# A prologue of its own for the first batch of a four-layer cross-attention kernel: the order of the first projections, the first maxima and the weights

## The chip, the core and the metric

The kernel runs on one core of a Trainium2 chip. The core has five engines, each with an instruction queue of its own: TensorE (PE, with its weight loads as PEld), VectorE (DVE), ScalarE (ACT), GpSimd (POOL) and SyncE (SP), which only issues DMAs here. ACT and POOL can issue DMAs too, and an issue takes its place in their queues. Every engine works through its queue in order and waits on semaphores for what another engine or a DMA has to deliver.

The metric is the time of one execution on the device in microseconds, the median of several runs. Profile times are microseconds from the start of the profiled span unless they are marked ns.

## The reference

`x` has shape (2, 1024, 288): two batches of 1024 tokens. It goes through two quantised layers, L0 and L1, and two plain layers, L2 and L3, which attend to 154 context rows. Only the beginning of L0 matters for this change:

```python
h = layer_norm(x, ln1_g, ln1_b, 1e-06)
q8, s, sm = quant_act(h)
q = quant_linear(q8, s, sm, wq1, bq1).reshape(b, n, H, D)   # H = 16 heads, D = 18
k = quant_linear(q8, s, sm, wk1, bk1).reshape(b, n, H, D)
v = quant_linear(q8, s, sm, wv1, bv1).reshape(b, n, H, D)
a = attn(q, k, v)
a8, sa, sma = quant_act(a)
x = x + quant_linear(a8, sa, sma, wo1, bo1)
...
```

`quant_act` rounds each token to integers in -127..127 by its own scale, and `quant_linear` quantises each weight row to 8 bits before it multiplies. A cross-attention and a feed-forward part follow in L0 and L1.

## The kernel before

**Tiles.** A batch has two halves of 512 tokens (`HQ`), each of four chunks of 128 tokens. The 16 heads are worked in four groups of four (`G`). One *step* of self-attention is one group of one half of one batch of one layer, so that there are 32 steps, eight for each batch of a layer.

**A step.** `self_maxima` (lines 558 to 585) finds the row maxima of the logits first: 32 units, each a matmul of 128 queries against 512 keys (line 564) and a DVE maximum over them (line 571). `store_maxima` (lines 530 to 552) splits the maxima into three bf16 parts on POOL, transposes them and puts them as extra rows into the query tile by a DMA that ACT issues. Only then can `attend` form the products: logits with the maxima already in them (`weights_unit`, line 623), the exponential on ACT (line 629) and the product with the values (line 653). `run` (line 783) lays the maxima of step i + 1 between the products of step i; the maxima of step 0 have nothing beside them.

**What a batch needs first.** `SelfAttention.prepare` (line 874) does for each half: `ln_quantise` (line 376: statistics on DVE, normalisation on ACT, the multiplication by g and addition of b on POOL at line 401, quantisation on DVE and ACT with small columns on POOL), `transposed`, `token_scales`, then keys, values and queries. Keys and queries go through `linear_T` (line 513), in three tiles of 108 features: three matmuls, a scaling on DVE (line 520), and `split` (line 473), which takes a number apart into three bf16 parts in the order ACT, POOL, ACT, POOL. `put` (line 492) writes the parts to DRAM, and `get_group` (line 504) reads them back, 72 features of a group at a time. The tile of the parts has two buffers.

**The order around the change.** The end of `tile_xattn` (lines 1427 to 1475) sets it. Before any step, three things are emitted to their end: `prep_a` (the norm's rows and the weights of keys, values and queries, line 832), `prep_a_out` (the output weight, line 841) and `layers[0].prepare()` (keys, values and queries of both halves). `self_attention` then fetches keys and two query tiles, and runs. All later work of other layers and batches is *side* work, which `beside` (line 1403) lays between the steps by weights: side work with weights of 118 in all, spread over 112 of the 128 yields of the first eight steps. The first entry of that side work is `layers[1].prepare()`, the second batch.

This order is only a priority. A planner (`schedule_with_timeline_sim`, line 56) simulates the engines and moves later work into gaps that it expects, within the limits of buffers and dependencies. The queues that the chip sees are its result.

**Loads.** SP issues all 16 chunks of `x` first (lines 109 and 110), and the weights and biases after them. POOL issues the context, the norm's rows and more. The rows of ones in the two key tiles `kT` are written by POOL (`head_rows`, line 87, called at line 1432).

Of the kernel before, what the change touches and what calls it, by code (L numbers as in the profile page):

```python
# [10 lines left out]
F32 = mybir.dt.float32  # L11
# [41 lines left out]
def tile_xattn(ctx: ExitStack, tc: tile.TileContext, ins: dict, out: bass.AP):  # L53
# [40 lines left out]

    def pair_rows(kt):

        ktv = kt.rearrange("p (q j) t -> p q j t", j=2)
        for q in range(H // 2):
            for n, (k0, k1) in enumerate(((0, NTXT), (NTXT, T))):
                nc.gpsimd.tensor_copy(  # L100
                    ktv[96:P, q, :, k0:k1],
                    ones22[96:P, :, n : n + 1].to_broadcast([P - 96, 2, k1 - k0]),
                )


# [3 lines left out]
    for n in range(NCH):  # L109
        nc.sync.dma_start(out=x[:, n, :], in_=xd[:, n, :])  # L110
# [168 lines left out]
    def prep(W, w_name, b_name, row0=0):  # L279
# [6 lines left out]
        nc.sync.dma_start(  # L286
# [8 lines left out]
    def prep_T(W, w_name, b_name, scaled=False):  # L295
# [6 lines left out]
        for n, f in enumerate(FT):  # L302
            nc.sync.dma_start(out=wv[:, n, :], in_=ins[w_name][f : f + FR, :])
# [72 lines left out]
    def ln_quantise(c0, ln, eps, s, name):  # L376
# [14 lines left out]
        h = view(big(f"{name}h"), c=HC, w=C)  # L391
# [8 lines left out]
        for j, op in ((0, ALU.mult), (1, ALU.add)):  # L400
            nc.gpsimd.tensor_tensor(
                h, h, ln[:, j : j + 1, :].to_broadcast([P, HC, C]), op
            )
        q = view(bf(f"{name}q")[:, 0 : HC * CZ], c=HC, w=CZ)
# [3 lines left out]
    def transposed(q, name):  # L408

        qT = view(bf(f"{name}qT")[:KZ], k=3, t=HQ)  # L410
# [62 lines left out]
    def split(y, bias, nt, name):  # L473

        st = work.tile([FR, 3, HQ], BF16, tag="parts", name=f"{name}st")[:, :, 0:nt]
        if bias is None:
            nc.scalar.copy(st[:, 0, :], y)
            nc.gpsimd.tensor_tensor(y, y, st[:, 0, :], ALU.subtract)
# [13 lines left out]
    def put(rows, st, n, nt):  # L492
        skip = 2 * D if n == 2 else 0
        nc.sync.dma_start(
# [18 lines left out]
    def linear_T(qT, w, sb, rows, name):  # L513

        qw, col = w
        for n in range(3):
# [6 lines left out]
            put(rows, split(y, None, HQ, name), n, HQ)  # L523
            yield 2
# [109 lines left out]

    def follow(one, other):

        one, other = (getattr(i, "ins", i) for i in (one, other))
        tc.add_manual_dep(
            one,
            other.name,  # L640
            mybir.DependencyInfo(
                mybir.DependencyClass.NoSync, mybir.DependencyReason.DATA
            ),
            reason="kept together",
        )
# [222 lines left out]
    class SelfAttention:  # L868
# [5 lines left out]
        def prepare(self):  # L874
            w, b, name = self.w, self.b, self.name
            self.k = [new_rows(f"{name}kr{hf}", "krows") for hf in range(2)]
            self.q = [new_rows(f"{name}qr{hf}", "qrows") for hf in range(2)]
            self.v = dram.tile([S // P, P, VW], F32, tag="vrows", name=f"{name}vr", bufs=2)
            for hf in range(2):
# [7 lines left out]
                yield from linear_T(qT, w["k"], sb, self.k[hf], f"{name}k")  # L887
                for c in range(HC):
                    n = hf * HC + c
                    v = vstage[n % 2]  # L890
                    quant_linear(
                        qT, c, w["v"], s[:, c : c + 1], v_heads(v), f"{name}v", heads
                    )
                    nc.sync.dma_start(out=self.v[n], in_=v)
                yield 3
                yield from linear_T(qT, w["q"], sb, self.q[hf], f"{name}q")
# [19 lines left out]
    def self_attention(layers):  # L916
# [18 lines left out]
        fetch(1)  # L935
        steps = []
        for n, (i, g, hf) in enumerate(order):
            L = layers[i]

            def pre(n=n, i=i, g=g, hf=hf, L=L):  # L940
                if g == 0:
# [40 lines left out]
        return run(steps)  # L982
# [23 lines left out]
    def cross_attention(w, b, name):  # L1006
# [38 lines left out]
        def queries(hf):  # L1045
# [7 lines left out]
            yield from linear_T(qT, w["q"], sb, rows[hf], f"{name}q")  # L1053
# [345 lines left out]
    def weighed(gen):  # L1399
        for _ in gen:  # L1400
            yield 1

# [24 lines left out]
    with tc.tile_pool(name="apool", bufs=1) as apool:  # L1427
        WA, WO = Weights(tpool, 1, 3, 1), Weights(apool, 1, 1, 1)
        kts = []
        for n, pool in enumerate((tpool, apool)):  # L1430
            kt = pool.tile([P, 4, S], BF16, name=f"kT{n}")
            head_rows(kt, 4, S)
            kts.append(kt)
        vstage = []
        for n in range(2):
# [6 lines left out]
        drain(prep_a(L0, wa[0]))  # L1442
        drain(prep_a_out(L0, wa[0]))
        drain(layers[0].prepare())
        main = self_attention(layers)
        sides = (
            (chain(layers[1].prepare(), prep_b(L0, wb[0]), prep_c(L0, wc[0])), 118),
# [21 lines left out]
        beside(main, 24, chain(islice(last, 2), weighed(islice(plain, 21))), 25, 24)  # L1469
# [47 lines left out]
```

## Time and profile before

| what | value |
|---|---|
| median of 3 runs | 2659.57 us (2655.34 to 2670.14) |
| the profiled execution, as timed | 2656.43 us |
| its profiled span | 2654.5 us |
| mean granted TensorE clock in it | 0.855 |
| PE busy in the span | 2057.5 us (78%) |
| DVE busy in the span | 1971.1 us (74%) |
| ACT busy in the span | 1409.9 us (53%) |
| POOL busy in the span | 819.3 us (31%) |
| first product of step 0 (line 623) starts | 160.9 us |
| first product of step 8 starts | 446.0 us |
| first product of step 16 starts | 954.5 us |

Busy times are the sums of an engine's instructions. Timeline rows read: start, length, engine, line, operation, written tile `<-` read tiles, shape, count; in brackets the idle time before it and what ended it. A row with a count above one is a merged run of neighbours. In names, `L_xattn_a` stands for the self-attention of any quantised layer, so that a row does not tell the batch or layer. In the window table each engine has its busy time and its count of instructions, followed by the granted TensorE clock, the busy share of the DMA engines and GB/s.

### The profile page before, as it was taken

The numbers are of one execution on the slowest core, as the hardware profiler recorded it, in microseconds if no ns is written. First come the engines' busy times: TensorE is split into PE (matmuls) and PEld (weight loads), VectorE is DVE, ScalarE is ACT, GpSimd is POOL, SyncE is SP. The second block draws the span as 40 slices with busy tenths as digits, with TensorE's granted clock in tenths as the row PEclk, the third lists the DMA queues.
The fourth block names the chain that finished last, engine by engine and source line by source line (L and its number), as shares of the span: only waits on it lengthen the run. The fifth ranks groups of instructions, "written<-read, shape, count | busy, mean of one in ns | idle before, by whom it ended". The sixth has DMA issues, their size and how long they took to land. (4 is left out here: it accounts for less than half of the span.)

```text
span 2654.5 us, 34216 instructions
## 1 busy us (share of the span) xinstructions
PE 2057.5 (78%) x10908; PEld 907.0 (34%) x10908; DVE 1971.1 (74%) x4512; ACT 1409.9 (53%) x2707; POOL 819.3 (31%) x1804
## 2 busy tenths in 40 slices
PE   1488998787884887788768677787767887778898
PEld 0223332323332333233333232323334433444444
DVE  6687888788888477888868958897357876655666
ACT  2346556555664755566656354466654544544443
POOL 7524212402124442022253440123264122413220
PEclk9779888789986888989868778798888977879999
DMA  3422201220000312110023121100033210112321
GB/s 88 122 70 86 57 22 49 77 55 17 27 11 20 119 44 78 42 29 21 6 83 94 31 80 34 33 23 12 25 82 101 74 28 25 51 40 67 86 66 36
DMA packets 158340, 140.27 MB, mean 53 GB/s; under 512 B 44251, under 2 KB 154164, under 8 KB 158161
## 3 DMA queue, kind: packets, MB, share of 16 engines
q1 hardware_dynamic: 147152, 118.67, 15.4%
q0 software_dynamic: 4864, 14.71, 2.3%
q10 hardware_dynamic: 6144, 4.72, 1.0%
q8 instruction: 86, 1.41, 0.2%
q14 instruction: 94, 0.76, 0.1%
HBM read 95.27 MB, written 38.04 MB: 50 GB/s over the span
## 5 line engine op out<-in xcount | busy, mean ns | idle before, releaser
L571 DVE TENSOR_REDUCE L_xattn_amxh<-L_xattn_amx 128x1 f32<-128x512 f32 x1024 | 670.9, 680 | 131.2 <-PE L_xattn_amx L564 123.7
L629 ACT ACTIVATE L_xattn_aatse<-L_xattn_aats 128x512 f32<-128x512 f32 x1024 | 556.1, 600 | 281.2 <-PE L_xattn_aats L623 245.1
L564 PE MATMUL L_xattn_amx<-kT,L_xattn_aqT 108*128 108x512 bf16 x1024 | 425.2, 433 | 122.1 <-DVE L_xattn_amxh L571 91.8
L623 PE MATMUL L_xattn_aats<-L_xattn_aqT,kT 120*128 120x512 bf16 x1024 | 374.7, 413 | 49.8 <-ACT L_xattn_aatse L629 33.4
L653 PE MATMUL L_xattn_aato<-L_xattn_aatse,L_xattn_av 128*32 128x512 f32 x2048 | 288.0, 634 | 22.1 <-ACT L_xattn_aatse L629 18.3
L629 ACT ACTIVATE L_xattn_atse<-L_xattn_ats 86x512 f32<-86x512 f32 (+1 forms) x256 | 139.7, 590 | 121.9 <-PE L_xattn_ats L623 98.5
L623 PEld LDWEIGHTS <-kT 120*128 120x128 bf16 x1024 | 98.9, 103 | 304.3 <-issue 262.0
L564 PEld LDWEIGHTS <-L_xattn_aqT 108*128 108x128 bf16 x1024 | 104.5, 105 | 266.7 <-issue 221.5
L627 DVE TENSOR_TENSOR L_xattn_batse<-L_xattn_bats,L_xattn_bmT 77x512 f32<-77x512 f32 x256 | 166.6, 676 | 37.1 <-PE L_xattn_bats L623 26.5
L629 ACT ACTIVATE L_xattn_batse<-L_xattn_batse 77x512 f32<-77x512 f32 x256 | 155.1, 622 | 37.8 <-DVE L_xattn_batse L627 32.2
L609 DVE TENSOR_REDUCE L_xattn_mxn<-L_xattn_mx 128x2 f32<-128x172 f32 (+1 forms) x512 | 129.3, 304 | 50.4 <-PE L_xattn_mx L594 48.3
L1280 PE MATMUL L_xattn_o<-wo,L_xattn_atp 128*128 128x288 f32 x512 | 143.7, 424 | 4.3 <-ACT L_xattn_mxsr L545 1.8
L604 DVE TENSOR_TENSOR L_xattn_bmxm<-L_xattn_bmx,L_xattn_bm 128x308 f32<-128x308 f32 x256 | 114.6, 464 | 30.8 <-PE L_xattn_bmx L594 25.8
L623 PE MATMUL L_xattn_bats<-L_xattn_bqT,L_xattn_bkT 120*77 120x512 bf16 x256 | 96.7, 433 | 42.0 <-DMA L_xattn_bqT<-L_xattn_bmxsr 29.0
L188 POOL CAST L_xattn_bmxst<-L_xattn_bmxn 128x16 bf16<-128x16 f32 x96 | 20.4, 212 | 345.4 <-DVE L_xattn_bmxn L609 176.2
L623 PE MATMUL L_xattn_ats<-L_xattn_qT,L_xattn_kT 120*86 120x512 bf16 (+1 forms) x256 | 92.5, 422 | 32.0 <-DMA L_xattn_qT<-L_xattn_mxsr 23.5
L609 DVE TENSOR_REDUCE L_xattn_bmxn<-L_xattn_bmxm 128x2 f32<-128x308 f32 x256 | 113.6, 458 | 0.8
L1280 PEld LDWEIGHTS L_xattn_o<-wo,L_xattn_atp 128*128 128x128 f32 x512 | 97.4, 196 | 38.1 <-DVE L_xattn_atp L764 3.6
L594 PE MATMUL L_xattn_mx<-L_xattn_kT,L_xattn_qT 108*128 108x154 bf16 x512 | 79.0, 257 | 26.3 <-DVE L_xattn_mxn L609 11.5
L594 PE MATMUL L_xattn_bmx<-L_xattn_bkT,L_xattn_bqT 108*128 108x154 bf16 x512 | 81.1, 261 | 21.7 <-DVE L_xattn_amxh L571 6.9
L653 PEld LDWEIGHTS L_xattn_aato<-L_xattn_aatse,L_xattn_av 128*32 128x32 f32 x2048 | 41.8, 110 | 155.8 <-ACT L_xattn_aatse L629 129.8
L594 PEld LDWEIGHTS <-L_xattn_bqT 108*128 108x128 bf16 x512 | 49.5, 110 | 99.3 <-issue 69.8
(558 smaller groups left out, 3848.6 us busy)
## 6 DMA issues: line engine op xcount, KB each, us to landing
kT<-L_xattn_akr SPq DMA_DIRECT2D x192, 72.0 KB
L_xattn_aqT<-L_xattn_aqr SPq DMA_DIRECT2D x192, 72.0 KB
L_xattn_bqT<-L_xattn_bqr SPq DMA_DIRECT2D x192, 72.0 KB
L_xattn_qT<-L_xattn_r SPq DMA_DIRECT2D x192, 72.0 KB
L_xattn_akr<-L_xattn_akst SPq DMA_DIRECT2D x16, 324.0 KB
L_xattn_aqr<-L_xattn_aqst SPq DMA_DIRECT2D x16, 324.0 KB
L_xattn_bqr<-L_xattn_bqst SPq DMA_DIRECT2D x16, 324.0 KB
L_xattn_r<-L_xattn_qst SPq DMA_DIRECT2D x16, 324.0 KB
```

Source lines behind the costliest of these rows:

```text
L188: eng.tensor_copy(part, r)
L564: nc.tensor.matmul(sp, lhsT=qt[:KR, j, c * P : (c + 1) * P], rhs=kt[:KR, j, a * 512 : (a + 1) * 512], start=True, stop=True,)
L571: nc.vector.tensor_reduce(halves[:, a, c, j, :], sp, AX.X, ALU.max, negate=True)
L594: nc.tensor.matmul(sp[:, j * T : (j + 1) * T], lhsT=qt[:KR, 2 * a + j, c * P : (c + 1) * P], rhs=kt[:KR, 4 * g + 2 * a + j, :], start=True ...
L604: nc.vector.tensor_tensor(lm, of, mask[:, c : c + 1, :].to_broadcast([P, 2, T]), ALU.add)
L609: nc.vector.tensor_reduce(nm[:, c, 2 * a : 2 * a + 2, n], of[:, :, k0:k1], AX.X, ALU.max, negate=True,)
L623: nc.tensor.matmul(sp, lhsT=keys(j), rhs=qt[:rows, j, :], start=True, stop=True)
L627: nc.vector.tensor_tensor(e, sp, maskT, ALU.add)
L629: nc.scalar.activation(e, src, AF.Exp)
L653: made = nc.tensor.matmul(po[32 * i : 32 * i + 32, :], lhsT=lhsT, rhs=rhs, start=start, stop=stop)
L1280: nc.tensor.matmul(ps, lhsT=pair[:, c * P : (c + 1) * P], rhs=wo[:, t0 + t, :], start=(t == 0), stop=(t == len(pairs) - 1),)
```

## The change

The first batch of L0 gets a method of its own, `prepare_first`, in place of `prep_a`, `prep_a_out` and `prepare`. It emits: the norm of half 0, the key weight, the transposes of half 0, the norm of half 1, the query weight, keys and queries of half 0, keys of half 1. What is left (`others`: value weight, values of both halves, queries of half 1) is laid between the 32 maxima of step 0, which now yield. The output weight becomes the first entry of the side work, whose weights rise from 118 to 126. Four things change for this batch alone:

- The norm's multiplication and addition and the subtractions in `split` are done by DVE (`nc.vector`) and not by POOL.
- The key and query weights are loaded through ACT's queue.
- The rows of ones in `kT` are written by ACT, eight copies of 32 x 1024.
- SP loads only the eight chunks of the first batch at the start. The second batch's eight chunks are placed behind the last `put` of the keys of half 1.

The norm's result and the transposed integers of this batch also live in other buffers (tags `a` and `qTb` in place of `big` and `bf`). The second query tile is fetched in step 0's `pre` and no longer before the first maxima.

```diff
+    def first_rows(kt):
+        for j in range(4):
+            nc.scalar.copy(kt[96:P, j, :], ones4[96:P, j : j + 1].to_broadcast([P - 96, S]))
...
-    for n in range(NCH):
-        nc.sync.dma_start(out=x[:, n, :], in_=xd[:, n, :])
+    def load_tokens(b, behind=None):
+        for n in range(b * 8, b * 8 + 8):
+            load = nc.sync.dma_start(out=x[:, n, :], in_=xd[:, n, :])
+            if behind is not None:
+                follow(load, behind)
+
+    load_tokens(0)
...
         for j, op in ((0, ALU.mult), (1, ALU.add)):
-            nc.gpsimd.tensor_tensor(
+            eng.tensor_tensor(
...
-            nc.gpsimd.tensor_tensor(y, y, st[:, 0, :], ALU.subtract)
+            eng.tensor_tensor(y, y, st[:, 0, :], ALU.subtract)
...
+        def prepare_first(self):
+            w, b, name = self.w, self.b, self.name
+            self.begin()
+            w["ln"] = load_ln(WA, L0, 1)
...
+            names = [(f"{L0}w{part}1", f"{L0}b{part}1") for part in "kqv"]
+            normalise(0)
+            w["k"] = prep_T(WA, *names[0], queue=nc.scalar)
+            qTs = [transposed(qs[0], f"{name}t", tile())]
+            normalise(1)
+            w["q"] = prep_T(WA, *names[1], scaled=True, queue=nc.scalar)
+            linear(0, "k", self.k)
+            linear(0, "q", self.q)
+            qTs.append(transposed(qs[1], f"{name}t", tile()))
+            load_tokens(1, linear(1, "k", self.k)[-1])
+
+            def others():
+                w["v"] = prep(WA, *names[2])
+                yield 8
+                for hf in range(2):
+                    self.values(hf, qTs[hf], scales[hf])
+                    yield 3
+                linear(1, "q", self.q)
+                yield 6
+
+            return others()
...
         fetch_keys(0)
         fetch(0)
-        fetch(1)
...
             def pre(n=n, i=i, g=g, hf=hf, L=L):
+                if n == 0:
+                    fetch(1)
...
-        return run(steps)
+        return run(steps, first=1)
...
-            head_rows(kt, 4, S)
+            first_rows(kt)
...
-        drain(prep_a(L0, wa[0]))
-        drain(prep_a_out(L0, wa[0]))
-        drain(layers[0].prepare())
+        others = layers[0].prepare_first()
         main = self_attention(layers)
+        beside(main, 33, others, 20, 30)
         sides = (
-            (chain(layers[1].prepare(), prep_b(L0, wb[0]), prep_c(L0, wc[0])), 118),
+            (
+                chain(
+                    prep_a_out(L0, wa[0]),
+                    layers[1].prepare(),
+                    prep_b(L0, wb[0]),
+                    prep_c(L0, wc[0]),
+                ),
+                126,
+            ),
```

In `prepare_first`, `normalise` calls `ln_quantise` and `linear` calls `token_scales` and `linear_T`, both with `nc.vector` in place of POOL. `values` holds the value loop that `prepare` had. `follow` orders two instructions without a semaphore.

## The prediction, made before the result was known

> **What bounds it now.** I read the sliced rows of the page first, then a table of windows, then the timeline of the first 161 us, because the change moves nothing else by hand.
>
> ```profile
> PE   1488998787884887788768677787767887778898
> DVE  6687888788888477888868958897357876655666
> ```
>
> Each digit is the tenth of a 66 us slice in which the engine is busy. From the third slice on PE is 80 to 90% busy; in the first it is under 20%, in the second under 50%. So the beginning has another limit than the rest. The windows are cut at its events:
>
> ```profile
> 0.00:60.00 60.00, 7.75 (x51) 6.23 (x51) 39.23 (x137) 11.27 (x26) 40.10 (x93) 1.00 0.43 97
> 60.00:132.40 72.40, 28.87 (x110) 17.35 (x110) 47.25 (x86) 23.02 (x48) 41.23 (x50) 0.75 0.39 111
> 132.40:154.20 21.80, 18.60 (x32) 3.37 (x33) 19.98 (x31) 2.47 (x4) 5.63 (x5) 0.50 0.35 104
> 154.20:160.90 6.70, 6.16 (x30) 3.82 (x30) 4.10 (x8) 2.90 (x8) 1.84 (x9) 0.54 0.05 10
> 160.90:446.00 285.10, 253.12 (x1318) 89.47 (x1317) 231.46 (x471) 166.24 (x325) 79.55 (x227) 0.89 0.20 58
> ```
>
> For 132 us no engine is over 67% busy: a chain of waits, not an engine, sets this stretch. Then 22 us belong to DVE alone (32 maxima at 0.68 us), 7 us are the latency of storing them, and the steps begin. There PE has 89% and DVE 81%. Now the chain:
>
> ```profile
> 67.66 5.18 POOL L401 TENSOR_TENSOR L_xattn_alh<-L_xattn_alh,L_xattn_ln 128x1152 f32<-128x1152 f32 x2
> 68.71 7.01 DVE L346 TENSOR_SCALAR L_xattn_ast<-L_xattn_alqs 128x4 f32<-128x4 f32 x1
> 122.36 0.35 SPq L494 DMA_DIRECT2D L_xattn_akr<-L_xattn_akst  x1
> 132.44 1.01 PE L564 MATMUL L_xattn_amx<-kT,L_xattn_aqT 108*128 108x512 bf16 x2 [4.87 <-DMA kT<-L_xattn_akr]
> ```
>
> POOL does eight norm operations (line 401, 2.61 us each) between 38.9 and 75.7 us, four for the second batch, which nobody needs yet. DVE stands in an operation of 0.17 us for 7.01 while they run, and the small columns behind them in POOL's queue hold the transposes until 81.8. The first tile of the second half's keys is put at 122.4, and the maxima start ten us later.
>
> **The first maxima.** *ACT before the norm:* a table load of 1.28 us, six weight DMAs at 0.79 (the price of line 549's issues in ACT's queue), eight copies of 32x1024, which have no row: copies of 512 and 768 columns took 0.58 and 0.79, so 0.82 ns a column, 1.0 us each. With 1.5 for the context copies, ACT is free at about 16 us and has normalised half 0 (four of 0.54) at 18.4. If the planner places the copies behind the norm, it is 12; if the g and b rows, which landed at 14 to 16, come later, 20.
>
> *DVE to the transposes:* multiplication and addition of 128x1152 have no DVE row; two-input operations of 308 and 512 columns took 464 and 676 ns, so 1.04 ns a column, 1.34 us each, against POOL's 2.61. Then maximum 1.35, scale 0.35, four scalings 1.21, the ACT tail 0.9 and sums 0.4: half 0 is quantised at 25.3. From transposes to the first scaling of a key tile it took 5.4 us (81.8 to 87.1), so that starts at 30.7, against 87.1.
>
> *DVE from 18.4 on:* two norms at 6.0; the query weight at 7.1 (two reductions 2.1, six scalings 2.5, ten small ones 1.6, three copies 0.9); nine tiles of k0, q0, k1 at 0.745 + 2 x 0.68 = 2.1, so 19.0. Sum 38.1, so 56.5 without a gap. The two buffers of parts limit too: a tile holds one for about 5.3 us, so nine tiles need 24 us from 30.7, to 55. With a tenth of gaps DVE ends at 60.7; the first tile of k1 is put two tiles earlier, at 56.5, and the ten us from put to maxima stay. **First maxima at 66 us, not 132.4**; bounds 58 (fewer gaps) and 80 (14 us of value and output weights in DVE's gaps, and the second batch's loads ahead of key reads in SP's queue, 8 x 0.4 us of issue and 1.18 MB at some 200 GB/s).
>
> **Two rules against it.** Six weight loads and eight token loads compete in the first 20 us, in which the table showed 197 GB/s with the DMA engines 91% busy. The Trainium skill ("DMA: Bandwidth & Descriptors", Issuing engines are not separate DMA queues) says that issuing from more engines saves the issue time only. By the row the key weight was ready at 24.4; by the rule it gains nothing from ACT's queue, but half of x goes away: 2.57 MB needed at 197 GB/s are there by 13 us. Either is met before the norm at 18.4 or costs at most 6 us. The second: VectorE operations with two SBUF inputs share an interface with GpSimd ("GPSIMD Engine Reference", Key points). All 28 moved operations are of this kind. By the row above, what holds DVE are the long POOL operations, and none is left ahead of the keys (the second batch's x isn't there): 0. By the rule each of POOL's small ones counts too, about 15 us in 60, over 21.6 us of moved work: 5 us. I keep it inside the tenth of gaps.
>
> **From the first maxima to the first products.** 32 maxima 21.9, eight value scalings 4.1, three tiles of q1 6.3: 32.3 us on DVE. The value weight (7.1) is on top only if it was not done in DVE's 15 idle us before 66; in the old trace it was done at 26 to 35, so I leave it out. PE at the granted 0.50 needs 32 x 0.43 + 6.5 for values + 3.9 for q1 + 2.8, 27 us: hidden, with little to spare. Storing is 6.7 as before. q1 is last in `others`, but ten maxima follow it, enough for its round trip through DRAM. **First products at 66 + 32 + 7 = 105, not 160.9: 56 us**, bounds 98 and 120, so 41 to 63.
>
> **What is owed later.** Up to 160.9 DVE was busy 39.2 + 47.3 + 20.0 + 4.1 = 110.6 us, 10.6 of it only held by POOL, so 100 of work, among it the output weight, the second batch's statistics and two weights of the cross-attention. The change adds 4 x 1.34 and 24 x 0.68 to DVE: 121.6. Up to 105 it can do some 94.5 (51 before 66 with the key weight and statistics, 7 value weight, 32, 4). So 27 us move into the steps. Their price is read from the steps of the first stage:
>
> ```profile
> 335.10:377.00 41.90, 36.25 (x174) 13.19 (x174) 38.04 (x88) 18.70 (x36) 13.24 (x58) 0.79 0.11 33
> 377.00:409.80 32.80, 30.11 (x159) 11.04 (x159) 21.58 (x39) 18.25 (x35) 1.08 (x5) 0.86 0.06 16
> ```
>
> A step with 16.5 us more DVE work is 9.1 longer: 0.55 per us; a line through all eight steps gives 0.6. So 27 us cost 16. Ends: 0.3 (8 us), if they fall into idle time, and 1.0 (27). POOL's four norm operations of the second batch now fall into the maxima or the steps and hold DVE there: eight held it 10.6 us, so four 5, at 0.6 another 3 (0 to 10). Moved PE work (9 transposes and 6 small matmuls of the output weight, some 3 us) is within the gaps. Two edits cost nothing: POOL loses the 7.2 us of key-tile rows and 28 operations, and had idle time in all stages; the second batch's keys are due only at step 8, 300 us later.
>
> **Sum:** 56 - 16 - 3 = 37 us. Against the profiled execution, 2656.4 (span 2654.5 and 1.9 around it), that is 2619; the median shown is 3 us above it, so I say 2620.
>
> **Rivals.**
> - *All is hidden (2604).* The owed DVE work costs 0.3 and the holds nothing: 58 - 8 = 50 to 55 us. For it: DVE idles 54 us in the first stage. Against: the slope of 0.6.
> - *The stretch stays long (2640).* The planner puts other weights, or the second batch's loads, ahead of the keys as it did with the norms: maxima at 85, products at 128, 33 - 16 = 17 us. For it: old DVE did two weights of the cross-attention at 88 to 130. Against: the worst of them needs tokens that now load behind the keys.
> - *The clock gives it back (2676).* In the first stage PE is granted 1.00, then 0.95, then 0.79. "TensorE: Matmul & The Clock Gate" (Part 1) ties the cold clock to idle windows of some 3.4 us; here it was 0.50 over 22 us in which PE was 85% busy, so that rule doesn't explain it. If the fall is a budget over time, 56 us less idling lowers the clock after. PE's 1996 busy us after 160.9 make 23 us per 0.01, about half on the path: 12. From a fall of 0.03 on the gain is gone; at 0.045 the loss is 54, 17 us more than the gain: 2676.
> - *No change.* The planner lays out all later work anew; old steps with like DVE work differ by 3 us (28.65 us of work: 32.7; 30.54: 36.2), so 32 steps can add or take about 12 us at random. With the long stretch this can cancel.
>
> **Chances.** Forecast 0.55, all hidden 0.15, long stretch 0.17, clock 0.08, no change 0.05. A measurement of this kernel tells about 0.5%, 13 us, from no change. Faster: 0.55 + 0.15 and 0.14 of the long stretch, 0.84; same: the rest of it and no change, 0.08; slower 0.08. The range takes the bounds 63 - 8 = 55 and 41 - 27 - 10 = 4 us of gain with the random part on the low side: 2592 to 2652.
>
> **What would show it.** Line 401 of this batch on DVE near 1.34 us and the subtractions near 0.7; the first maxima matmul near 66 and its run of maxima about 32 us long; the first product near 105; step 8 near 446 - 37 = 409; from there each stage as long as before (508 and 550 us), mean clock within 0.01 of 0.855. Wrong, if the first product is before 98 or after 120, if the first stage grows by more than 27 us over 285, or if a later stage moves by more than 12.

## The result, and the profile after

The changed kernel takes **2626.88 us** (median of 4 runs, 2626.06 to 2628.85) where the kernel before, run beside it, takes 2657.45 (4 runs, 2646.99 to 2670.14). The medians lie 30.6 us apart; the ratio of the runs on record is **0.9894, 95% interval 0.9865 to 0.9923**, so the kernel is about 1.1% faster. The profiled execution took 2626.06 us (span 2624.2) against 2656.43 (span 2654.5), at the same mean granted clock, 0.855. Line numbers below are those of the changed kernel: the norm's multiplication and addition stand at line 424 (401 before), the statistics' shift at 410, the subtractions of `split` at 505 and 512, `put` at 521, `get_group` at 533, the maxima at 595 (matmul) and 602 (reduction), and the logits of the products at 654.

One slip has to be told first. The description of the change and the prediction say that both subtractions of `split` go to DVE, 24 of them. Only the first of the two does (line 505, 12 operations); the second, line 512, stays on POOL. So DVE was given 12 x 0.68, some 8 us, less than the prediction gave it.

The sliced rows of the page, PE and DVE busy tenths in 40 slices of 65.6 us:

```profile
PE   2599888787884887787779678787768887879988
DVE  6777878788898487998768958987346896656666
```

In the second slice PE now has 5 tenths and in the third 9: the steps begin earlier. The window table, cut at the changed kernel's events, has for each engine busy us and (instructions), then granted clock, DMA share and GB/s:

```profile
0.00:29.80 29.80, 2.77 (x18) 2.10 (x18) 15.40 (x62) 10.22 (x13) 14.05 (x29) 1.00 0.68 149
29.80:54.50 24.70, 5.58 (x33) 4.57 (x34) 22.41 (x65) 10.00 (x26) 16.58 (x57) 1.00 0.04 8
54.50:89.40 34.90, 21.11 (x89) 12.70 (x89) 16.51 (x26) 14.38 (x24) 13.69 (x24) 0.66 0.46 142
89.40:136.40 47.00, 23.28 (x56) 7.43 (x57) 42.85 (x97) 10.53 (x23) 19.09 (x17) 0.57 0.49 139
136.40:142.90 6.50, 5.04 (x20) 1.91 (x20) 5.92 (x12) 0.57 (x1) 1.09 (x5) 0.50 0.06 10
142.90:435.90 293.00, 261.24 (x1341) 93.86 (x1341) 234.40 (x487) 169.72 (x331) 82.56 (x233) 0.87 0.20 56
435.90:935.90 500.00, 385.42 (x2081) 159.05 (x2081) 397.34 (x857) 297.58 (x573) 153.29 (x301) 0.84 0.16 47
935.90:1419.80 483.90, 382.03 (x2091) 156.78 (x2091) 399.70 (x858) 298.50 (x572) 147.13 (x304) 0.86 0.18 50
1419.80:2624.00 1204.20, 961.88 (x5198) 467.60 (x5197) 828.45 (x2069) 608.78 (x1154) 354.40 (x817) 0.86 0.18 50
```

The cuts are: the norm starts on ACT (29.8), the first key matmul (54.5), the first maxima matmul that needs both halves (89.4), the operation that joins the maxima of step 0 (line 607, 136.4), the first product (142.9), and the first products of steps 8, 16 and 24. The same later stages before:

```profile
446.00:954.50 508.50, 390.30 (x2087) 158.41 (x2087) 404.24 (x863) 297.31 (x573) 151.16 (x301) 0.84 0.16 46
954.50:1447.30 492.80, 382.45 (x2084) 156.50 (x2084) 395.99 (x852) 298.14 (x572) 147.41 (x304) 0.86 0.18 49
```

| us | before | after | gain so far |
|---|---|---|---|
| norm starts on ACT | 35.9 | 29.8 | 6.1 |
| first key matmul | 86.2 | 54.5 | 31.7 |
| first full maxima | 132.4 | 89.4 | 43.0 |
| maxima of step 0 end | 154.3 | 136.4 | 17.9 |
| first product | 160.9 | 142.9 | 18.0 |
| first product of step 8 | 446.0 | 435.9 | 10.1 |
| of step 16 | 954.5 | 935.9 | 18.6 |
| of step 24 | 1447.3 | 1419.8 | 27.5 |
| end of span | 2654.5 | 2624.2 | 30.3 |

So the prologue wins 43 us up to the maxima, loses 25 of them while the maxima run, loses 8 more in the first eight steps, and then two stages that the change does not touch by hand win 8.5 and 8.9, and the rest 2.8. The size of the forecast came out; its path did not.

**Why the keys came at 54.5 and not at 31.** Timeline of DVE in the changed kernel (start, length, line, operation; in brackets the idle time before and its releaser), and of POOL and of ACT's and SP's queues, second fence:

```profile
13.03 0.46 DVE L403 BATCH_NORM_STATS2 L_xattn_alst<-x 128x6 f32<-128x288 f32 x1 [1.63 <-DMA x<-in_x_dram]
...
17.58 0.46 DVE L403 BATCH_NORM_STATS2 L_xattn_alst<-x 128x6 f32<-128x288 f32 x1 [3.76 <-DMA x<-in_x_dram]
...
20.87 1.05 DVE L221 TENSOR_REDUCE L_xattn_wq1s<-L_xattn_wq1w 108x3 f32<-108x864 f32 x1 [2.69 <-DMA L_xattn_wq1b<-in_L_xattn_bq_dram]
...
23.00 0.45 DVE L403 BATCH_NORM_STATS2 L_xattn_alst<-x 128x6 f32<-128x288 f32 x1
...
28.61 1.11 DVE L239 TENSOR_SCALAR L_xattn_wq1w<-L_xattn_wq1w,L_xattn_wq1s 108x288 f32<-108x288 f32 x3
29.63 0.23 DVE L410 SCALAR_TENSOR_TENSOR L_xattn_alsh<-L_xattn_almv,L_xattn_alr 128x4 f32<-128x4 f32 x2
32.03 4.05 DVE L424 TENSOR_TENSOR L_xattn_ah<-L_xattn_ah,L_xattn_ln 128x1152 f32<-128x1152 f32 x3 [2.18 <-ACT L_xattn_ah L416]
...
44.65 1.04 DVE L222 TENSOR_REDUCE L_xattn_wo_0s<-L_xattn_wo_0w 96x3 f32<-96x864 f32 x1
```

```profile
13.97 1.04 POOL L408 TENSOR_TENSOR L_xattn_alr<-L_xattn_alr,neghalf 128x4 f32<-128x4 f32 x1 [1.36 <-DVE L_xattn_alr L405]
...
4.69 0.31 ACTq L325 DMA_DIRECT2D L_xattn_wq1w<-in_L_xattn_wq_dram  x1
9.45 2.15 ACTq L325 DMA_DIRECT2D L_xattn_wq1w<-in_L_xattn_wq_dram  x2
8.49 8.44 SPq L296 DMA_DIRECT2D L_xattn_wk1b<-in_L_xattn_bk_dram  x3
20.39 0.72 SPq L296 DMA_DIRECT2D L_xattn_wq1b<-in_L_xattn_bq_dram  x2
```

The shift of the norm (line 410, 0.23 us for two) waits for nothing but its turn. Its last input for half 0, a power on POOL (line 408), ends at 15.0, but in DVE's queue the shift stands behind the work on both weights, and that work waited in turn for its loads: at 17.58 for tokens, at 20.87 for the query weight. The releaser printed there is the query *bias*, but the reduction (line 221) reads only the weight, and two of the three bias loads were not issued before 20.39. In the packet records of the trace the last packet of the query weight, in ACT's queue, ends at 20.1 us, and the last of the tokens at 19.6. So two things came together, late loads and a norm that stands behind them though it needs only the first tokens. In the first 20 us 3.65 MB moved, needed or not, at 182 GB/s; the prediction had 2.57 MB, there by 13 us. u1 below has the other order: there the shift runs at 14.4.

Then the planner put the value and output weights (lines 221 to 239 of `wv_0` and `wo_0`, 40.6 to 54.2 us) between the quantisation of the halves.

**Why the maxima took 47 us and not 32.** Timeline of the changed kernel's maxima, POOL and DVE:

```profile
103.28 10.34 POOL L424 TENSOR_TENSOR L_xattn_alh<-L_xattn_alh,L_xattn_ln 128x1152 f32<-128x1152 f32 x4 [1.28 <-ACT L_xattn_alh L416]
114.90 2.60 POOL L512 TENSOR_TENSOR L_xattn_aqst<-L_xattn_aqy,L_xattn_aqst 108x512 bf16<-108x512 f32 x2 [1.27 <-ACT L_xattn_aqst L511]
```

```profile
107.83 1.05 DVE L221 TENSOR_REDUCE L_xattn_wq2s<-L_xattn_wq2w 108x3 f32<-108x864 f32 x1 [2.24 <-DMA L_xattn_wq2w<-in_L_xattn_wq_dram]
...
111.01 3.16 DVE L505 TENSOR_TENSOR L_xattn_aqy<-L_xattn_aqy,L_xattn_aqst 108x512 f32<-108x512 f32 x1
...
115.30 1.11 DVE L223 TENSOR_TENSOR L_xattn_wq2s<-L_xattn_wq2s 108x3 f32<-108x3 f32 x1
```

DVE is busy for 42.9 of these 47 us. The window's 97 instructions are not only the 32 maxima, four value scalings and the queries: the planner fetched the second batch's statistics and norm (36 instructions, 12.8 us by the sum of their lengths) and a weight of the cross-attention (`wq2`, 19 instructions, 7.2 us) into it. While POOL multiplies and adds for that norm (until 113.6), a subtraction of 0.69 us lasts 3.16; beside POOL's second subtraction of `split` (line 512) an operation of 0.15 us lasts 1.11. The first of these is the mechanism which the change took out of the beginning, back in another place.

### The profile page after: what moved, and what is told of

Its sections match the earlier page's. It is cut to its first block, busy times and chain, and to the rows that moved or that the text cites. A ratio compares the mean times of both kernels' runs of the same rounds, so it can differ in the third digit from the quotient of the medians.

```text
span 2624.2 us, 34259 instructions
## 1 busy us (share of the span) xinstructions
PE 2048.4 (78%) x10924; PEld 906.0 (35%) x10924; DVE 1963.0 (75%) x4528; ACT 1420.3 (54%) x2717; POOL 801.9 (31%) x1786
## 5 line engine op out<-in xcount | busy, mean ns | idle before, releaser
L654 PE MATMUL L_xattn_aats<-L_xattn_aqT,kT 120*128 120x512 bf16 x1024 | 375.7, 414 | 49.9 <-ACT L_xattn_aatse L660 30.3
L625 PE MATMUL L_xattn_mx<-L_xattn_kT,L_xattn_qT 108*128 108x154 bf16 x512 | 77.2, 254 | 27.6 <-DVE L_xattn_mxn L640 10.2
```

Source lines behind the costliest of these rows:

```text
L625: nc.tensor.matmul(sp[:, j * T : (j + 1) * T], lhsT=qt[:KR, 2 * a + j, c * P : (c + 1) * P], rhs=kt[:KR, 4 * g + 2 * a + j, :], start=True ...
L654: nc.tensor.matmul(sp, lhsT=keys(j), rhs=qt[:rows, j, :], start=True, stop=True)
```

## The experiments

Every kernel here does all of the computation. "Key matmul" is the first matmul with the key weight, "full maxima" the first maxima matmul that needs both halves' keys, "maxima end" the start of the operation that joins the maxima of step 0. "Prologue" is the time to the first product, "stage 1" the first eight steps, "stages 2 + 3" the next sixteen. Times are medians, ratios are to the kernel before in the same batch of runs, other columns from one profile each.

| run | us | ratio, 95% | key matmul | full maxima | maxima end | prologue | stage 1 | stages 2 + 3 |
|---|---|---|---|---|---|---|---|---|
| before | | | 86.2 | 132.4 | 154.3 | 160.9 | 285.1 | 1001.3 |
| after | 2626.88 | 0.9894 (0.9865–0.9923) | 54.5 | 89.4 | 136.4 | 142.9 | 293.0 | 983.9 |
| e1, before again | 2657.93 | 1.001 (0.9994–1.0025) | 86.9 | 132.9 | 154.7 | 161.5 | 284.5 | 1002.2 |
| e2, weights later | 2631.08 | 0.991 (0.9885–0.9936) | 49.3 | 89.7 | 135.8 | 142.9 | 291.5 | 990.3 |
| e3, tokens later | 2625.08 | 0.9894 (0.9846–0.9942) | 55.9 | 93.0 | 126.1 | 145.3 | 285.0 | 982.9 |
| e4, both later | 2612.19 | 0.9842 (0.9799–0.9884) | 50.5 | 91.0 | 126.7 | 135.8 | 295.9 | 983.8 |
| u1, old buffers | 2636.85 | 0.9934 (0.9909–0.9958) | 52.4 | 96.5 | 141.0 | 147.7 | 289.5 | 992.2 |
| u2, arithmetic on POOL | 2623.95 | 0.9868 (0.98–0.9935) | 55.9 | 98.3 | 147.2 | 153.8 | 289.7 | 980.7 |
| u3, weights by SP | 2630.02 | 0.99 (0.9856–0.9944) | 55.8 | 92.9 | 138.9 | 145.7 | 290.0 | 980.1 |
| u4, rows by POOL | 2633.24 | 0.9908 (0.9863–0.9952) | 55.4 | 95.2 | 142.2 | 149.5 | 289.3 | 980.4 |
| u5, tokens at start | 2622.70 | 0.9867 (0.9821–0.9913) | 65.4 | 110.6 | 139.3 | 146.3 | 291.1 | 983.7 |
| u6, others first | 2628.53 | 0.9889 (0.985–0.9928) | 54.6 | 91.8 | 138.7 | 145.6 | 290.4 | 994.0 |
| p5, five parts buffers | 2629.97 | 0.9895 (0.9859–0.993) | 55.2 | 92.9 | 132.4 | 139.2 | 292.3 | 997.4 |
| b6, e4, p5 and line 512 on DVE | 2634.85 | 0.9907 (0.9875–0.9939) | 49.7 | 84.7 | 120.4 | 129.2 | 305.6 | 992.9 |

One caution for all rows: executions of one kernel differ by up to 25 us (the kernel before, 27 runs beside e1 to e4: 2646.43 to 2671.37; e3: 2611.9, its profiled one, to 2628.65), so a profile's span can differ from its median by 13 us, and some medians rest on two runs (u2, u5, u6, p5). Changed kernels whose medians lie a few us apart are not told apart.

**e1: is the later gain in the kernel or in the run?** The kernel before once more, no edit.

> The kernel before, profiled once more. Only 18 of the 30 us that the change gained are there at the first product (142.9 for 160.9); step 0 to 8 gives 8 back, steps 8 to 16 and 16 to 24 win 8.5 and 8.9. Scatter theory: the later 17 are scatter of one execution, so here steps 8 to 16 and 16 to 24 again differ from 508.5 and 492.8 by several us, towards 500 and 484. Plan theory: they belong to the new order of the queues, so here they come out within 2 us of 508.5 and 492.8, and the first product within 1 us of 160.9.

Every point of the prologue and each stage came back within 2.5 us (stages 284.5, 507.0, 495.2; 285.1, 508.5, 492.8 before); stage 3 moved by 2.4, a little more than the plan theory allowed, and stages 2 and 3 together by 0.8. So the 17 us that they gain belong to the changed program and not to the scatter of an execution.

**e2: the value and output weights behind the first keys.** Their loads are ordered behind the first `put` of the keys in SP's queue:

```diff
-        queue.dma_start(
+        load = queue.dma_start(
...
+        if behind is not None:
+            follow(load, behind)
...
-            linear(0, "k", self.k)
+            self.put = linear(0, "k", self.k)[0]
...
-                w["v"] = prep(WA, *names[2])
+                w["v"] = prep(WA, *names[2], behind=self.put)
...
-                    prep_a_out(L0, wa[0]),
+                    prep_a_out(L0, wa[0], layers[0].put),
```

> Changed kernel; loads of value and output weight placed behind the first put of keys, so that their 11 us of DVE work leave 40 to 54 us and fall among the key and query tiles. Queue theory (the planner's order on DVE holds the keys): first full maxima at 78 to 82 instead of 89.4, first product about 8 earlier, time 4 to 8 us less. Latency theory (loads, parts buffers and the ACT-DVE-POOL chain of each tile set it): the tiles take as long as before or longer, first maxima 86 to 92, time within 3 us.

The keys start 5.2 us earlier, so the weights did stand in their way; the full maxima come at 89.7 all the same. The same weight work now lies between keys and maxima: DVE has 27.56 us busy there and not 16.51, up to the maxima 56.1 and 54.3. Taking the weights from ahead of the keys gains nothing at the maxima, as the latency theory had it.

**e3: the second batch's tokens behind the last queries of half 1**, not behind its keys, to keep the second batch's work out of the maxima.

```diff
-            load_tokens(1, linear(1, "k", self.k)[-1])
+            linear(1, "k", self.k)
...
-                linear(1, "q", self.q)
+                load_tokens(1, linear(1, "q", self.q)[-1])
```

> Changed kernel; the second batch's token loads placed behind the last put of the queries of half 1 instead of the keys, so that its statistics, norm and POOL's four long operations leave the maxima of step 0. Queue theory: the stretch of maxima is 35 to 38 us instead of 47, first product near 132; the moved work (some 12 us of DVE, 10 of POOL) costs 4 to 8 in steps 0 to 7, so the time is 2 to 7 us less. Latency theory: maxima are held by waits for loads and queries; first product 139 to 144, time the same or more by what moved.

The maxima shrink from 47.0 to 33.1 us. The second batch's statistics still lie in them (20 instructions, 5.5 us); its norm and `wq2`, which the edit does not name, are out. But the first product comes 19.2 us after their end where it took 6.5, at 145.3 and not near 132 or, by the other theory, 139 to 144. The timeline of that gap, POOL, DVE and PE:

```profile
126.29 0.21 POOL L210 CAST L_xattn_amxst<-L_xattn_amxn 128x16 bf16<-128x16 f32 x1 [0.81 <-DVE L_xattn_amxn L607]
...
127.03 2.62 POOL L424 TENSOR_TENSOR L_xattn_alh<-L_xattn_alh,L_xattn_ln 128x1152 f32<-128x1152 f32 x1
...
129.60 0.23 POOL L212 TENSOR_TENSOR L_xattn_amxn<-L_xattn_amxn,L_xattn_amxst 128x16 f32<-128x16 f32 x1
129.78 5.18 POOL L424 TENSOR_TENSOR L_xattn_alh<-L_xattn_alh,L_xattn_ln 128x1152 f32<-128x1152 f32 x2
...
134.92 0.21 POOL L210 CAST L_xattn_amxst<-L_xattn_amxn 128x16 bf16<-128x16 f32 x1
...
135.59 2.11 DVE L328 TENSOR_SCALAR L_xattn_wq2col<-L_xattn_wq2s 108x3 f32<-108x3 f32 x1
...
139.60 0.59 PE L570 MATMUL L_xattn_amxspt<-ident,L_xattn_amxst 128*12 128x128 bf16 x4
...
145.27 1.44 PE L654 MATMUL L_xattn_aats<-L_xattn_aqT,kT 120*128 120x512 bf16 x3 [3.98 <-DMA L_xattn_aqT<-L_xattn_amxsr]
```

The small operations that split the maxima (0.2 us each) stand in POOL's queue behind the norm of the second batch: 127.03 to 129.6 and 129.78 to 134.9. Their transposes (line 570) then wait until 139.60 in PE's queue, behind maxima of step 1 whose reductions wait behind held DVE operations (0.14 us lasts 1.98 from 133.02 and 2.11 from 135.59). Wherever the norm was put in these runs, it held what was due beside it. The loss at the first product is not a loss at step 8: that starts at 430.3, the earliest of all rows, since stage 1 took 285.0 us (293.0 in the changed kernel, and 4 to 8 more were expected).

**e4: e2 and e3 together.**

> Changed kernel with the loads of value and output weight and the second batch's tokens both placed later. Queue theory: first product near 122 to 126, steps 0 to 8 longer by 6 to 10, time 6 to 14 us less than the changed kernel. Latency theory: first product 137 to 144, time within 4 us.

Its window table, key matmul to full maxima, maxima, storing, first eight steps:

```profile
50.50:91.00 40.50, 19.85 (x78) 11.71 (x77) 27.57 (x60) 14.26 (x24) 20.10 (x43) 0.64 0.41 119
91.00:126.70 35.70, 24.24 (x68) 8.98 (x69) 29.50 (x61) 4.29 (x7) 3.80 (x3) 0.60 0.63 187
126.70:135.80 9.10, 7.74 (x29) 3.55 (x28) 8.68 (x20) 5.12 (x10) 8.19 (x10) 0.50 0.04 7
135.80:431.70 295.90, 257.25 (x1334) 89.40 (x1334) 244.60 (x520) 171.25 (x338) 90.07 (x243) 0.89 0.21 58
```

The first product, 135.8, lies between the two theories' ranges; the time, 14.7 us below the changed kernel's by the medians, is that of the queue theory or a little better. The first product comes 7.1 us before that of the changed kernel, and stage 1 has 10.2 us more DVE work and is 2.9 us longer; step 8 starts at 431.7, 4.2 earlier. It has the lowest median of all, 2612.19 (4 runs, 2608.74 to 2619.56), and beats the kernel before by 1.6%. The interval of its ratio overlaps that of the changed kernel by a little, and 13 of the 17 us between the two spans lie behind step 24, 10.8 of them in step 27 (78.1 us and 88.9). That step takes 78 to 79 us in u2, u5 and u6 too and 83 to 92 in all others; whether the program or the execution decides it was not settled. That e4 is better than the changed kernel is likely, by how much is open.

**u1: h and the integers in the buffers of before.**

```diff
-                    c0, w["ln"], 1e-6, s, f"{name}l", h, tile(), nc.vector
+                    c0, w["ln"], 1e-6, s, f"{name}l", None, None, nc.vector
...
-            qTs = [transposed(qs[0], f"{name}t", tile())]
+            qTs = [transposed(qs[0], f"{name}t")]
```

> Changed kernel with the norm's result and the integers of the first batch back in the buffers of before (big and bf). The queues from L0's cross-attention on then stand nearly as before the change (95.5% of DVE's instructions in the same order; the changed kernel 88.7%). Plan theory: steps 8 to 24, 983.8 us in the changed kernel and 1001.3 before, take 994 to 1003 here. Start theory (the later gain comes from what the new prologue leaves behind, whatever the order): 980 to 988. First product 142 to 150 by both.

The shift of half 0 now stands ahead of the weights in DVE's queue and runs at 14.40. The norm starts at 14.6, 15 us earlier, and the keys at 52.4, only 2 earlier. The timeline on DVE and ACT, POOL and PE shows what took its place:

```profile
14.40 0.15 DVE L410 SCALAR_TENSOR_TENSOR L_xattn_alsh<-L_xattn_almv,L_xattn_alr 128x4 f32<-128x4 f32 x1
14.59 2.18 ACT L416 ACTIVATE L_xattn_alh<-x,L_xattn_alsh,L_xattn_alr 128x288 f32<-128x288 f32 x4 [0.95 <-DVE L_xattn_alsh L410]
18.41 1.47 ACTq L325 DMA_DIRECT2D L_xattn_wk1w<-in_L_xattn_wk_dram  x3
```

```profile
31.12 0.19 POOL L254 TENSOR_TENSOR L_xattn_wk1s<-L_xattn_wk1b,L_xattn_wk1s 108x3 f32<-108x3 f32 x1 [15.54 <-DVE L_xattn_wk1col L328]
```

```profile
42.21 0.43 PE L286 MATMUL L_xattn_wk1pt<-ident,L_xattn_wk1sq 108*100 108x108 bf16 x3 [3.68 <-DVE L_xattn_wk1t L289]
```

The load of the key weight is now issued behind the norm in ACT's queue, and its quantisation, not the norm, is late. Norm and weight are two chains into the same matmul; advancing one leaves the other. Stages 2 and 3 take 992.2 us, in neither theory's range but half way between the 984 and 1001 that they had started from; the first product, 147.7, is in the range.

**u2 to u4: one part of the change undone each.** u2 puts the norm's and the split's arithmetic back on POOL (`nc.vector` to `nc.gpsimd` in `normalise` and `linear`), u3 loads the weights by SP, u4 lets POOL write the rows of ones:

```diff
-            w["k"] = prep_T(WA, *names[0], queue=nc.scalar)
+            w["k"] = prep_T(WA, *names[0])
...
-            first_rows(kt)
+            head_rows(kt, 4, S)
```

> Changed kernel with the first batch's norm and first subtraction back on POOL. Queue theory: four norm operations at 2.61 for 1.34 and nine subtractions at 1.15 for 0.69 lengthen the way to the maxima by 5 to 10 us: first maxima 95 to 100, first product 149 to 155. Latency theory: hidden behind loads and parts buffers, first product 141 to 146.

> Changed kernel with the key and query weights loaded by SP again, behind the tokens. Order of all queues from the cross-attention on is that of the changed kernel, so steps 8 to 24 take 981 to 987. Load theory (weights by ACT's queue are there sooner and that counts): first product 147 to 153. Queue theory: the norm's shift waits behind the weights' DVE work anyway, first product 139 to 146.

> Changed kernel with the key tiles' rows of ones on POOL again (7.2 us). Both theories: POOL's square root of half 0 moves from 14 to some 18 us, but the norm starts at 29.8, so first product 142 to 145 and steps 8 to 24 as in the changed kernel, 981 to 987.

u2 puts the full maxima at 98.3 and the first product 10.9 us later, at 153.8, as its queue theory said: of the three edits this one costs most there. Yet its total is not worse: stage 1 is 3.3 us shorter, stages 2 and 3 another 3.2. u3 costs 2.8 us at the first product (145.7, in the range of its queue theory), so the issuing queue is small. u4 costs 6.6, where 2 at most were expected: its keys are 0.9 later, and from there to the full maxima it takes 39.8 us for 34.9 with the same DVE work (16.9 and 16.5). Why was not followed up; 2.9 us of it are left at step 8 (438.8).

**u5: all tokens at the start**, as before the change.

```diff
     load_tokens(0)
+    load_tokens(1)
...
-            load_tokens(1, linear(1, "k", self.k)[-1])
+            linear(1, "k", self.k)
```

> Changed kernel with all 16 token loads at the start again. Queue theory: the planner again finds the second batch's statistics and norm ready early and puts them ahead of the first batch's keys, POOL's four long operations hold DVE as before the change: first maxima 100 to 110, first product 150 to 158. Latency theory: only 1.18 MB more in the first 20 us: first maxima 92 to 96, first product 140 to 147. Steps 8 to 24 981 to 987 by both, since the later order is that of the changed kernel.

The full maxima come 21.2 us later and end only 2.9 later. Its window table, key matmul to maxima and maxima:

```profile
65.40:110.60 45.20, 21.59 (x88) 13.07 (x87) 30.92 (x61) 18.10 (x36) 23.05 (x37) 0.59 0.46 128
110.60:139.30 28.70, 22.43 (x59) 7.19 (x60) 25.67 (x43) 4.29 (x7) 3.75 (x3) 0.62 0.52 157
```

The second batch's statistics and norm are done ahead of the maxima, which then last 28.7 us. The queue theory's delay came at the full maxima (110.6), but not at the first product, 146.3, which is in the range of the latency theory. Holding the tokens back moved that work from one side of the maxima's start to the other: about half of the 43 us won at that start were this, and 3.4 of the 18 won at the first product. In the total no loss is seen (2622.70, two runs).

**u6: the others not interleaved by hand.** `drain(others)` ahead of the steps and an empty side stream in its place.

```diff
-        beside(main, 33, others, 20, 30)
+        drain(others)
+        beside(main, 33, iter(()), 20, 30)
```

> Changed kernel with value weight, values and queries of half 1 emitted before the maxima of step 0 and nothing beside them. Queue theory: the maxima take 22 us again and start about as much later as the work beside them weighed (10 us of values and queries): first maxima 100 to 106, first product 146 to 152 if the second batch's work stays beside the maxima, near 135 if it doesn't. Steps 8 to 24, in an order 96.5% that of before, 990 to 1002. Rival: the interleaving is what gave the 18 us; first product 155 to 161.

The full maxima come at 91.8, earlier than either theory had them, and the first product at 145.6, 2.7 us later than in the changed kernel and just under the queue theory's range; the rival's is out. Stages 2 and 3, 994.0, are in their range. The planner lays the value work and the last queries into the maxima by itself; emitting them there is worth little.

**p5: five buffers of parts and not two**, for every second of the first nine tiles, in room that the query tiles have free.

```diff
-        st = work.tile([FR, 3, HQ], BF16, tag="parts", name=f"{name}st")[:, :, 0:nt]
+        if st is None:
+            st = work.tile([FR, 3, HQ], BF16, tag="parts", name=f"{name}st")[:, :, 0:nt]
...
+            def room():
+                turns.append(0)
+                if len(turns) > 9 or len(turns) % 2:
+                    return None
+                return query_tile(f"{name}st", "qT")[:FR, 0:3, :]
```

> Changed kernel in which every second of the first nine key and query tiles takes its parts from a free query tile, five buffers in place of two. Latency theory of the tiles (a tile's parts are held until its put has landed, so that the next casts wait, 3.3, 2.5, 0.7, 2.4 and 1.7 us in the changed kernel): the way from the first key matmul to the first maxima, 34.9 us, shrinks to 25 to 29, first maxima 80 to 84. Queue theory (DVE's order sets it): 33 to 36, first maxima 88 to 91. First product earlier by what the first maxima gain, at most.

From the key matmul to the full maxima it takes 37.7 us, with two buffers 34.9: longer than in either theory. More buffers, which the prediction named as a limit, did not shorten that way. The first product is 3.7 us earlier, as less of the second batch's work came into the maxima (16 instructions for 36), and the later stages have an order of their own, so the edit changes more than the buffers.

**b6: e4, p5 and line 512 on DVE** (`nc.gpsimd` to `eng`). The last of the three is what the prediction had described; no run makes that edit alone.

> The kernel with both groups of loads later (2612 us), with five buffers of parts for the first nine tiles and the second subtraction of split on DVE as well (0.69 for 1.15 us). If both waits are on the path, the first product comes at 124 to 130 for 135.8, and the time is 2602 to 2608 us. If the queues' order alone counts, first product 133 to 138 and 2609 to 2616.

The earliest first product of all, 129.2, as expected if both waits are on the path; but the time, 2634.85, is 19 us above the higher of the two ranges and 23 above e4's; of the 31 us between the two profiles 18.5 lie behind step 24. It has the longest first stage, 305.6 us, with 255.6 us of DVE work; step 8 starts at 434.8, 1.1 before the changed kernel's. What DVE did not do ahead of the first product it does behind it: 342.0 us up to step 8 before, 337.5 after, 339.1 in e4, 346.7 in b6. u2 has 331.2, since POOL does its part.

**The order in the later stages.** The built programs were compared for the share of DVE's instructions, from L0's cross-attention to L1's, that stand in the same order. e3, e4, u3, u4 and u5 have the changed kernel's order (share 1.000) and need 980.1 to 983.8 us for stages 2 and 3, whenever their first product comes (135.8 to 149.5). The kernel before has a share of 0.887 and 1001.3. Others with their own order (0.835 to 0.929) lie at 980.7 (u2) and at 990.3 to 997.4. So the later gain goes with the planner's new order, not with the earlier start, at least for starts from 135.8 to 149.5. Likeness of order alone does not give it: u1 and u6, with 0.955 and 0.965 in the order of the kernel before, are 7 to 9 us faster than it in these stages. Which placements make the 17 us was not tested; in the profiles it is many small waits (step 19: 68.9 to 64.6 us), and no edit here can hold the order and change one of them.

## Why the prediction was right, and where it was not

The time (2620 forecast, 2626.88 measured), the direction and the range held. That is luck: the prologue gained 38 us less than forecast (18 for 56), and the first stage gave back 11 less (8 for 19) while the later stages gained 20, which the prediction had only as a random term of about 12 with either sign. By its own signs the prediction was wrong: the first product came after 120. Term by term:

| step of the prediction | predicted | measured |
|---|---|---|
| norm operation, subtraction on DVE | 1.34, 0.68 us | 1.35 (4.05 for three), 0.69 |
| half 0 normalised by ACT | 18.4 | 31.9 (starts at 29.8) |
| from there to the first scaling of a key tile | 12.3 | 23.9 |
| first scaling of a key tile | 30.7 | 55.8 |
| from there to the full maxima | 35.3 | 33.6 |
| first full maxima | 66 (58 to 80) | 89.4 |
| maxima | 32 | 47.0 |
| storing | 7 | 6.5 |
| first product | 105 (98 to 120) | 142.9 |
| growth of stage 1 | 16 + 3 | 7.9 |
| later stages | 0, 12 at random | 20.2 shorter |
| mean clock | within 0.01 | 0.855, the same |

- **"ACT is free at about 16 us and has normalised half 0 at 18.4": the step that failed first.** The sum followed ACT and the sizes of DVE's operations, and asked of the loads only how many bytes share the DMA engines. It did not ask what stands ahead of the shift in DVE's queue: two weights' work that waits for its own loads. The two bounds given, 12 and 20, left that out. "2.57 MB needed at 197 GB/s are there by 13 us" was mis-sized too: the query weight was there at 20.1. "Either is met before the norm at 18.4 or costs at most 6 us" fell with both; the norm was 13.5 us late, and the other 11.6 us up to the first scaling are work that the planner put between: half 1's norm and the value and output weights, of which e2 gives back 5.2.
- **"14 us of value and output weights in DVE's gaps"** was part of the upper bound, and came true; e2 shows that moving them behind the keys gains nothing at the maxima. This is the rival of the long stretch, which put the maxima at 85 and the product at 128: its place was right, and it was still short, since
- **"32.3 us on DVE"** for the maxima counted only work that step 0 owns. u5, where nothing else lies in the stretch, takes 28.7 us; with the three value scalings that it had done earlier and the three second subtractions that stayed on POOL (1.5 and 2.0 us) that is the sum. The rest of the 47.0 is the second batch's work and the cross-attention's weight, 12.8 and 7.2 us. e3's 33.1 is close to the forecast partly by chance: 5.5 us of it are the second batch's statistics. The prediction had seen the danger ("POOL's four norm operations of the second batch now fall into the maxima or the steps and hold DVE there") and priced it at 3 us behind the first product.
- **"27 us move into the steps ... cost 16"** was too large in its amount. DVE's work in stage 1 grew by 2.9 us only, since the prologue stayed long enough to do the rest, and since 12 subtractions, some 8 us, stayed on POOL. PE's grew by 8.1 us, as much as the stage; its idle time was 32.0 us before and 31.8 after. Part of that is moved work that had been put "within the gaps": PE has 3.6 us less ahead of the first product and 23 more matmuls behind it. Part is the clock of that stage, 0.87 for 0.89: u3 to u6, with as much work, have 0.90, PE busy for 255.4 to 256.7 us and stages of 289.3 to 291.1. As to the price, where DVE was made to owe more, e4 (13.1 us over before) has a stage longer by 10.8 and b6 (24.1) by 20.5: some 0.8 for each us, not the 0.6 of the slope. These are two rows; those with 2 to 4 us more than before have stages from 285.0 to 293.0 us, so the price is known only roughly.
- **"32 steps can add or take about 12 us at random"**: the term was right in kind, the planner's new order, and its size was 20. It is not random from run to run, as e1 shows, and why it was a gain here and not a loss was not found.
- **The two rules** cost little. With the weights loaded by SP the first product is 2.8 us later (u3), and the nine moved subtractions ahead of the full maxima last 0.68 to 0.69 us, but for two of 1.09 and 1.23. POOL's hold came behind them, in the maxima.
- **The clock that gives it back** did not come: 0.855 before and after.

Most of what a kernel gains at its first product it gives back by step 8. Across the fourteen rows of the table the first product lies between 129.2 and 161.5 and step 8 between 430.3 and 446.0; for first products between 129.2 and 146.3 step 8 lies at 430.3 to 437.5 in no order, and only later ones push it on, to 443.5 in u2.

## What to carry to other kernels

A start that is set by waits is not shortened by the sum of the work on its path: ask, for each instruction of the path, what the planner has put ahead of it in its queue and what that waits for, and expect free time to be filled with later work. When the same work has to be done before a later point, compare kernels at that later point (here step 8), not at the first event. With a planner, a change in the beginning lays out the rest anew; here that was worth 20 us where the beginning itself was worth 10 at step 8, and the old kernel, profiled twice, shows that it is not noise. And a releaser that a profile prints is an inference: compare it with what the instruction reads and with when the transfers ended.

## What the runs showed of the hardware

POOL's and DVE's holds work both ways. While DVE ran three norm multiplications (4.05 us from 32.03, 128 x 1152 with two operands from SBUF), POOL's copies of three columns took 1.3 us and not 0.19:

```profile
33.41 0.19 POOL L212 TENSOR_TENSOR L_xattn_wq1s<-L_xattn_wq1s,L_xattn_wq1sq 108x3 f32<-108x3 f32 x1
33.56 1.32 POOL L210 CAST L_xattn_wk1sq<-L_xattn_wk1s 108x3 bf16<-108x3 f32 x1
34.81 1.33 POOL L210 CAST L_xattn_wq1sq<-L_xattn_wq1s 108x3 bf16<-108x3 f32 x1
36.08 0.19 POOL L210 CAST L_xattn_wk1sq<-L_xattn_wk1s 108x3 bf16<-108x3 f32 x1
```

1.3 us is the length of one of DVE's operations (1.35): the small copy lasts as long as the operation beside it.

The other unexpected number is the 8.44 us that three bias loads of 0.4 KB needed to be issued by SP straight after the tokens (three others of the same line took 1.34 us at 23.45). It goes with the time and not with the loads: the DMA engines were busy for all of 4 to 17 us (0.96 to 1.02 by the windows), and in u3 three weight loads in that place took 6.61 us from 7.09, in u1 the query biases 7.40 from 7.47, while in u5 the same key biases, issued at 23.34, took 1.22. What holds the queue in a busy stretch was not tested.
